# Cross-attention's 64-column products in one row per unit, contexts first in the last units

## The chip, the cores and the metric

The kernel runs on one core of a Trainium2 chip. The core has TensorE (PE: matmuls, and beside them a loader of weights), VectorE (DVE), ScalarE (ACT), GpSimd (POOL) and SyncE (SP), which issues most DMAs. They run at the same time and wait for each other by semaphores; each takes its instructions in the order in which they are queued. The metric is the device time of one execution in microseconds, the median of several runs.

## The reference, cut to what matters

A pre-norm decoder layer on x of 16 sequences of 64 tokens and 256 columns, with three parts, each added to x:

```python
x = x + self_attention(layernorm(x), ...)           # 16 heads of 128, weights as codes times scales
x = x + cross_attention(layernorm(x), ctx_512, ...)  # latent attention, below
x = x + moe(layernorm(x), ...)                       # 16 experts, 4 per token, and a shared one
```

The cross-attention, per head h of 16 (K = 128, latent query 192 wide, context 64 wide, R = 64):

```python
q_hk  = (hidden_q @ Wq.T).reshape(B, S, H, K)
q_big = rope(einsum('bshk,hkq->bshq', q_hk, w_kc_q))       # 192 wide
kv_r  = rope(kv_c)
q_r   = einsum('bshq,hqr->bhsr', q_big, W_qr)
k_r   = einsum('bld,hdr->bhlr', kv_r, W_kr)
attn  = softmax(einsum('bhsr,bhlr->bhsl', q_r, k_r))
ctx_c = einsum('bhsl,bld->bhsd', attn, kv_r)
ctx   = einsum('bhsd,hkd->bhsk', ctx_c, w_kc_kv)
return ctx.transpose(0, 2, 1, 3).reshape(B, S, H * K) @ Wo.T
```

The expert layer takes a softmax over 16 logits, picks two of four groups of experts and then four experts per token, and adds their weighted outputs and a shared expert's.

## The kernel before

**Tiling.** The 1024 tokens are eight tiles x[0] to x[7] of 128 tokens; half 0 is the first four, half 1 the rest. After a layer norm, `layernorm_t` (L159) leaves a half's rows transposed, two 128-row chunks of 512 tokens, each split in a high and a low part for float precision; a product over such parts is three matmuls (`three`, L107). PSUM has four buffers "mm", two "at" and two "av", each one bank.

**Cross-attention.** Heads go in four quads, and a quad for one half of the tokens is a unit; there are eight, in the list `units` (L1134). `quad_steps` (L403) multiplies a quad's weights together ahead of time (matmuls L431, L453, L470); for quads 2 and 3 that happens inside the units' loop, as the generator `prep`. A unit is then:

- `rotated_queries` (L975), a generator in three steps t=0, 1, 2. Each step makes two products of six matmuls of 128 columns into an mm buffer (helper line L104, called "w_q work" here, 12 matmuls a step), four multiplications by the rope table on DVE (L993, the "factors", rt), which empty the buffers, and a subtraction and an addition on POOL (L999), which make two tiles of rotated rows, `roped`.
- `pair_queries` (L1005): the queries of four heads from all six roped tiles, on 64 columns of the array per product (L1014; 24 matmuls in the trace), into two mm buffers, copied to `q_r` by ACT (L1025).
- `pair_scores` (L1029), twice, two heads each: 16 matmuls of 64 columns (L1037) into an at buffer, then `softmax` (L320): maximum, difference, (ACT) exponential, sum, reciprocal on DVE, and the final multiplication on POOL (L334), or on DVE for the last unit.
- `transposed` (L339), twice: four PE transposes (L343) and two ACT copies.
- `pair_context` (L1046), twice: 16 matmuls of 64 columns (L1050) into an av buffer, split in parts c_t by ACT (L112) and DVE (L113).
- `cross_project` (L1064): four products of six matmuls (L104, w_o), one mm buffer each, added to x by DVE (L1075).

**Staging.** The loop over n (L1138) is a software pipeline: iteration n does the rotation of unit n, the queries and scores of unit n−1, and the transposes, contexts and projection of unit n−2. Half 0 of x is complete after n=6; a third layer norm and the routing follow there: `choose(0)` (L760) is two short groups of matmuls and a long row of small DVE operations, and `send` (L846) scatters rows by POOL's DMAs. After n=9 the same is done for half 1, with the shared expert's products (`shared_up`, L909, and others) as PE's filler; then come the routed experts, whose first input rows need these sends.

**Order.** No order is written out by hand. A planner with a model of durations takes the instructions as the program issues them, earlier ones first where several are ready, and so fixes each engine's queue. `tc.issue_after(ins)` (in `after`, L95) makes instructions of the block stand behind `ins` in the queue of ins's engine, without a wait. `behind` (L249) makes a true wait on semaphores.

Of the kernel before, what the change touches and what calls it, by code (L numbers as in the profile page):

```python
# [30 lines left out]
ALU = mybir.AluOpType  # L31
# [40 lines left out]
def decoder_layer(ctx: ExitStack, tc: tile.TileContext, a: dict, out: bass.AP):  # L72
    nc = tc.nc
# [11 lines left out]
    def mm_tile(rows=128, cols=512):  # L85
        return ps_mm.tile([128, 512], F32, tag="mm", name="mm")[:rows, :cols]
# [15 lines left out]
    def matmuls(ps, pairs):  # L102
        for n, (l, r) in enumerate(pairs):
            m = nc.tensor.matmul(ps, lhsT=l, rhs=r, start=(n == 0), stop=(n == len(pairs) - 1))  # L104
        return m.ins
# [43 lines left out]
    n_pt, pn_turned = [0], []  # L149
# [99 lines left out]
    def behind(read, writes):  # L249
        for w in writes:  # L250
            tc.add_manual_dep(
                read,
                w.name,
                mybir.DependencyInfo(mybir.DependencyClass.Sync, mybir.DependencyReason.DATA),
                reason="it reads rows of each",
            )
# [58 lines left out]
    with ExitStack() as attn:  # L315
# [4 lines left out]
        def softmax(sc, scale, eng=None):  # L320

            shape = [128, 8, S]
            m = small.tile([128, 8], F32, tag="sm_m", name="sm_m")
            nc.vector.tensor_reduce(m, sc, AX.X, ALU.max)  # L324
            p = soft.tile(shape, F32, tag="p", name="p")
            nc.vector.tensor_tensor(p, sc, m.unsqueeze(2).broadcast_to(shape), ALU.subtract)  # L326
            exps.append(nc.scalar.activation(p, p, AF.Exp, scale=scale).ins)  # L327
            s = small.tile([128, 8], F32, tag="sm_s", name="sm_s")
            nc.vector.tensor_reduce(s, p, AX.X, ALU.add)  # L329
            nc.vector.reciprocal(s, s)  # L330
            pn = soft.tile(shape, F32, tag="pn", name="pn")
            softened.append(
                (eng or nc.vector)
                .tensor_tensor(pn, p, s.unsqueeze(2).broadcast_to(shape), ALU.mult)  # L334
                .ins
            )
            return pn
# [153 lines left out]
        with tc.tile_pool(name="sw", bufs=2, side="right") as sw, tc.tile_pool(name="sa", bufs=2, side="right") as sa:  # L491
# [143 lines left out]
            for h in range(NH + 3):  # L635
# [9 lines left out]
                last = []  # L645
# [86 lines left out]
        def token_rows(half):  # L732
            return [rows[half][k // 2][:, k % 2, :D] for k in range(4)]
# [234 lines left out]
        with (  # L968
# [3 lines left out]
            def rope_table(t, k):  # L972
                return rope_q[:, t, k : k + 1, :].broadcast_to([128, 8, S])

            def rotated_queries(w_q, half, roped):  # L975
                for t in range(3):
                    m = []
                    for ab in range(2):
                        ps = mm_tile()
                        cols = slice(t * 128, (t + 1) * 128)  # L980
                        pairs = []
                        for c in range(2):
                            pairs += three(
                                [w[:, c, ab, cols] for w in w_q],
                                [p[:, c, :] for p in xn_t[half]],
                            )
                        matmuls(ps, pairs)
                        ps3 = ps.rearrange("p (b s) -> p b s", s=S)
                        for k in range(2):
                            mt = xa.tile(  # L990
                                [128, 8, S], F32, tag=f"rt{ab}{k}", name=f"rt{ab}{k}"
                            )
                            nc.vector.tensor_tensor(mt, ps3, rope_table(t, 2 * ab + k), ALU.mult)  # L993
                            m.append(mt)
                    for ab, (one, two, op) in enumerate(
                        ((m[0], m[3], ALU.subtract), (m[2], m[1], ALU.add))
                    ):
                        r = xa.tile([128, 512], F32, tag=f"roped{t}{ab}", name=f"roped{t}{ab}", bufs=1)
                        nc.gpsimd.tensor_tensor(  # L999
                            r.rearrange("p (b s) -> p b s", s=S), one, two, op  # L1000
                        )
                        roped.append(r)
                    yield

            def pair_queries(w_s, roped):  # L1005
                ps = [mm_tile() for _ in range(2)]
                left = [4 if h in (1, 2) else 2 for h in range(4)]
                first = [True] * 4
                for t in range(3):
                    for ab in range(2):  # L1010
                        for blk in range(2):
                            h = BLOCK_HEADS[t][blk]
                            left[h] -= 1
                            nc.tensor.matmul(  # L1014
                                ps[h // 2][(h % 2) * 64 : (h % 2) * 64 + 64],
                                lhsT=w_s[:, t, blk, ab, :],
                                rhs=roped[2 * t + ab],
                                start=first[h],
                                stop=left[h] == 0,
                            )  # L1020
                            first[h] = False
                q_rs = []
                for pr in range(2):
                    q_r = xa.tile([128, 512], F32, tag="q_r", name="q_r", bufs=2)
                    nc.scalar.copy(q_r, ps[pr])  # L1025
                    q_rs.append(q_r)
                return q_rs

            def pair_scores(q_r, half, eng):  # L1029

                sc = at_tile([128, 8, S])
                sc4 = sc.rearrange("p (h g) s -> p h g s", h=2)
                for g in range(2):
                    for pp in range(2):
                        for par in range(2):
                            b = 4 * g + 2 * par + pp
                            nc.tensor.matmul(  # L1037
                                sc4[par * 64 : par * 64 + 64, :, 2 * g + pp, :],
                                lhsT=q_r[:, b * S : (b + 1) * S],
                                rhs=kv_bd[:, half * 8 + b],  # L1040
                                start=True,
                                stop=True,
                            )
                return softmax(sc, 1.0, eng)

            def pair_context(pt, half):  # L1046
                av = av_tile()
                for k in range(4):
                    for hp in range(2):
                        nc.tensor.matmul(  # L1050
                            av[hp * 64 : hp * 64 + 64, k * 128 : (k + 1) * 128],
                            lhsT=kv[:, half * 4 + k, :],
                            rhs=pt[:, 4 * hp + k].rearrange("p a q -> p (a q)"),
                            start=True,
                            stop=True,
                        )
                c_t = [
                    xa.tile([128, 512], F32R, tag=f"c_t{n}", name=f"c_t{n}", bufs=4)
                    for n in range(2)
                ]  # L1060
                parts_of(av, c_t[0], c_t[1])
                return c_t

            def cross_project(w_o, c_ts, half, last):  # L1064
                for k in range(4):
# [69 lines left out]
            late = {1: quad_steps(2, weights, xb), 3: quad_steps(3, weights, xw)}  # L1135
            prep = iter(())
            roped, pns = {}, {}
            for n in range(len(units) + 2):  # L1138
                here = range(len(units))
                if n in late:  # L1140
# [2 lines left out]
                roped[n] = []  # L1143
                qd, half = units[min(n, len(units) - 1)]
                rotate = iter(rotated_queries(weights[qd][0], half, roped[n]) if n in here else ())
                pts_n = [transposed(pn) for pn in pns.pop(n - 2, ())]
                if n - 1 in here:
                    q_rs = pair_queries(weights[units[n - 1][0]][1], roped.pop(n - 1))
                c_ts = [pair_context(pt, units[n - 2][1]) for pt in pts_n]
                next(rotate, None)  # L1150
                if n - 1 in here:

                    eng = nc.gpsimd if n < len(units) else nc.vector
                    pns[n - 1] = [pair_scores(q_rs[0], units[n - 1][1], eng)]
                if n in late:
                    next(prep)
                next(rotate, None)
                if n == 0:
                    with tc.issue_after(highs[-1]), tc.issue_after(lows[-1]):
                        xn_t += layernorm_t(2, (1,))  # L1160
                if n - 1 in here:
                    pns[n - 1].append(pair_scores(q_rs[1], units[n - 1][1], eng))
                if n in late:
                    next(prep)
                if n - 2 in here:
# [24 lines left out]
                    )  # L1190
                if n == 6:
                    rows[0] = [raw_tile(tag, [128, 2, ROW]) for tag in ("wq", "wkq")]
                    normed[0] = layernorm_t(3, (0,), token_rows(0))[0]
                if n == 7:
                    choose(0)
                    send(0, (0, 1))
# [333 lines left out]
```

## Time and profile before

| | |
|---|---|
| median of 3 runs | 562.55 us (560.79 to 564.96) |
| the profiled execution, its own time | 559.35 us |
| its span | 557.5 us |
| PE, weight loader | 526.9 us (95%), 440.0 us (79%) |
| DVE, ACT, POOL | 398.9 us (72%), 276.9 us (50%), 230.3 us (41%) |
| mean granted PE clock | 0.984 |
| cross-attention, by the first and last of its matmuls | 204.4 to 409.2 us |

A span is counted from the first instruction of the trace to the last, and times in the text are from its start. Busy time of PE is that of matmuls in flight, which overlap: a matmul of 512 columns is recorded with about 0.40 us, while the next starts 0.23 us after it. So what tells a lost moment on PE is the distance between starts. "Issue" is a wait that the profile has no releaser for. In rows, "128\*64" is the part of the array that a matmul uses, rows by columns.

### The profile page before, as it was taken

What the parts mean: (1) busy time and instruction counts of PE and PEld (TensorE: products, weight loads), DVE (VectorE), ACT (ScalarE), POOL (GpSimd) and SP (SyncE); (2) the same over time, 40 slices, a digit from 0 to 9 for tenths busy, and PEclk for the clock granted to TensorE, in tenths of its full rate; (3) what the DMA queues carried; (4) which work ended last, traced back from release to release, by engine and by line L of the source; (5) the groups of instructions that cost most, each with busy time, mean ns of one, the idle gap of its engine ahead of it and who ended that gap; (6) DMA issues with size and microseconds to landing.
All of it is one profiled execution on the core that took longest, in us unless ns stands there. A gap on an engine that the chain in (4) does not pass through costs nothing.

```text
span 557.5 us, 10620 instructions
## 1 busy us (share of the span) xinstructions
PE 526.9 (95%) x4013; PEld 440.0 (79%) x4013; DVE 398.9 (72%) x879; ACT 276.9 (50%) x524; POOL 230.3 (41%) x213
## 2 busy tenths in 40 slices
PE   7999999999999989999999999999999789999961
PEld 6898898998999965756778577685788679999951
DVE  5464574664746888846768496889778679999776
ACT  4677557576574511321332323143535468776551
POOL 4360510210101015516344443642545737888862
PEclk9999999999999999999999999999999989999995
DMA  8453431923201889280020000010512677676375
GB/s 255 152 178 108 126 104 54 235 86 115 77 1 37 263 240 288 80 243 13 1 68 6 8 1 1 0 31 1 166 67 83 208 252 252 233 251 227 136 258 176
DMA packets 44262, 70.83 MB, mean 127 GB/s; under 512 B 11824, under 2 KB 25232, under 8 KB 44208
## 3 DMA queue, kind: packets, MB, share of 16 engines
q1 hardware_dynamic: 39376, 58.71, 34.8%
q0 software_dynamic: 3696, 10.36, 4.8%
q10 hardware_dynamic: 1136, 1.05, 0.6%
q8 instruction: 33, 0.54, 0.4%
q14 instruction: 21, 0.17, 0.1%
HBM read 48.61 MB, written 21.86 MB: 126 GB/s over the span
## 4 chain that ended last, share of the span: by engine, by line
PE 77%; DVE 9%; POOL 4%; issue 3%; DMA 3%; ACT 3%; SPq 0%; DVEq 0%; POOLq 0%; ACTq 0%
PE mm L104 45%; PE mm L1014 7%; PE av L592 5%; PE av L104 3%; PE at L573 3%; PE at L343 3%; PE at L1037 2%; POOL xd L851 2%; PE av L1050 2%; PE mm L431 2%; PE mm L453 1%; ACT w L278 1%; DMA got<-yd 1%; DVE x L1343 1%; PE at L1274 1%
## 5 line engine op out<-in xcount | busy, mean ns | idle before, releaser
L999 POOL TENSOR_TENSOR roped<-rt,rt 128x512 f32<-128x512 f32 x48 | 62.6, 1325 | 83.0 <-DVE rt L993 80.1
L993 DVE TENSOR_TENSOR rt<-mm,rope_q 128x512 f32<-128x512 f32 x96 | 61.4, 685 | 24.1 <-PE mm L104 23.6
L104 PE MATMUL mm<-xn,w_q 128*128 128x512 f32 x288 | 73.9, 403 | 0.5 <-ACT xn L222 0.5
L104 PEld LDWEIGHTS mm<-xn,w_q 128*128 128x128 f32 x288 | 52.2, 188 | 14.0 <-issue 1.8
L104 PE MATMUL mm<-xs,w 128*128 128x384 f32 x270 | 54.2, 348 | 5.0 <-ACT xs L112 2.7
L1313 POOL DMA_INDIRECT yd<-y,to x45 | 47.8, 1062 | 20.8 <-ACT y L1308 8.3
L104 PEld LDWEIGHTS mm<-xs,w 128*128 128x128 f32 x270 | 47.0, 193 | 7.2 <-ACT xs L112 3.7
L324 DVE TENSOR_REDUCE sm_m<-at 128x8 f32<-128x512 f32 x32 | 21.8, 680 | 43.1 <-PE at L573 42.2
L1014 PE MATMUL mm<-roped,w_s 128*64 128x512 f32 x192 | 46.4, 602 | 0.7 <-POOL roped L999 0.7
L514 POOL TENSOR_TENSOR wv<-code,scale 128x512 fp32r<-128x512 f32 x7 | 10.3, 1471 | 88.4 <-DMA code<-in_codes 45.2
L327 ACT ACTIVATE p<-p 128x512 f32<-128x512 f32 x32 | 20.4, 636 | 38.6 <-DVE p L326 38.6
L329 DVE TENSOR_REDUCE sm_s<-p 128x8 f32<-128x512 f32 x32 | 21.9, 683 | 21.1 <-ACT p L327 21.1
L104 PE MATMUL mm<-wv,xn 128*128 128x256 f32 x256 | 36.2, 289 | 0.0
L104 PE MATMUL av<-w,hp 128*128 128x256 f32 x225 | 35.1, 289 | 0.4 <-ACT y L1308 0.3
L104 PE MATMUL mm<-xn,wk 128*128 128x512 f32 x128 | 34.3, 399 | 0.0
L351 ACT COPY pt<-at 64x512 f32<-64x512 f32 x32 | 18.5, 579 | 30.8 <-PE at L343 30.7
L104 PE MATMUL mm<-xn,wq 128*128 128x512 f32 x128 | 33.2, 398 | 0.2
L104 PEld LDWEIGHTS mm<-wv,xn 128*128 128x128 f32 x256 | 32.5, 189 | 0.7
L104 PE MATMUL mm<-wo,o 128*128 128x256 f32 x256 | 33.0, 285 | 0.0
L601 ACT ACTIVATE o<-av,bqkv 128x512 fp32r<-128x512 f32 x32 | 21.3, 688 | 23.0 <-PE mm L104 19.0
L1014 PEld LDWEIGHTS mm<-roped,w_s 128*64 128x64 f32 x192 | 13.9, 136 | 22.9 <-issue 20.5
L104 PEld LDWEIGHTS mm<-wo,o 128*128 128x128 f32 x256 | 31.4, 191 | 0.7 <-issue 0.4
(216 smaller groups left out, 1169.1 us busy)
## 6 DMA issues: line engine op xcount, KB each, us to landing
w<-in_W SPq DMA_DIRECT2D x15, 640.0 KB, 4.3
code<-in_codes SPq DMA_DIRECT2D x32, 256.0 KB, 4.5
scale<-in_scales SPq DMA_DIRECT2D x32, 256.0 KB, 4.8
xr<-xd SPq DMA_DIRECT2D x15, 408.0 KB, 4.8
xd<-zeros SPq DMA_DIRECT2D x8, 720.0 KB, 7.1
yd<-zeros SPq DMA_DIRECT2D x8, 512.0 KB, 6.8
got<-yd SPq DMA_DIRECT2D x16, 256.0 KB, 3.8
wq<-in_Wq SPq DMA_DIRECT2D x4, 512.0 KB, 4.6
```

The source lines that it names most:

```text
L104: m = nc.tensor.matmul(ps, lhsT=l, rhs=r, start=(n == 0), stop=(n == len(pairs) - 1))
L324: nc.vector.tensor_reduce(m, sc, AX.X, ALU.max)
L327: exps.append(nc.scalar.activation(p, p, AF.Exp, scale=scale).ins)
L329: nc.vector.tensor_reduce(s, p, AX.X, ALU.add)
L343: last = nc.tensor.transpose(ps[:, 2 * n : 2 * n + 2, :].rearrange("p a q -> p (a q)"), pn[:, 2 * n : 2 * n + 2, :].rearrange("p a k -> p ...
L351: nc.scalar.copy(pt[:S, :, 0, :], ps[:S])
L592: nc.tensor.matmul(av[:, k * 128 : (k + 1) * 128], lhsT=v[:, i, k0 : k0 + HD], rhs=pt[:, i].rearrange("p a q -> p (a q)"), start=True, sto ...
L601: nc.scalar.activation(o[0][:, cols], av, AF.Identity, bias=bias)
L993: nc.vector.tensor_tensor(mt, ps3, rope_table(t, 2 * ab + k), ALU.mult)
L999: nc.gpsimd.tensor_tensor(r.rearrange("p (b s) -> p b s", s=S), one, two, op)
L1014: nc.tensor.matmul(ps[h // 2][(h % 2) * 64 : (h % 2) * 64 + 64], lhsT=w_s[:, t, blk, ab, :], rhs=roped[2 * t + ab], start=first[h], stop=l ...
L1313: sent = nc.gpsimd.indirect_dma_start(out=yd[: (E - 1) * SLOTS + min(TOPK, E - 1 - e) * NT], out_offset=bass.IndirectOffsetOnAxis(ap=to[:, ...
```

## The change

In each iteration the order of PE's work is now bound:

1. The transposes of unit n−2 stand behind the last projection product of the iteration before (for n < 8).
2. t=0 of unit n's rotation comes first; the queries of unit n−1 stand behind its last matmul and (n > 2) behind the transposes. The first query product also waits, truly, for the last DVE factor of unit n−1 (`roped_done`; not in n=8).
3. The contexts of unit n−2, both, stand behind the queries; both scores behind the contexts; preparation and t=1 behind the scores. Before, the scores of the two pairs had t=1 between them, and the planner was free.
4. For n = 7 and above contexts come ahead of the queries. The layer norm of half 0 for the experts moves from the end of n=6 to n=7, behind these contexts.

```diff
@@ rotated_queries @@
-                        matmuls(ps, pairs)
+                        asked = matmuls(ps, pairs)
...
-                            nc.vector.tensor_tensor(mt, ps3, rope_table(t, 2 * ab + k), ALU.mult)
+                            factors = nc.vector.tensor_tensor(
+                                mt, ps3, rope_table(t, 2 * ab + k), ALU.mult
+                            )
...
-                    yield
+                    roped_last[0] = factors.ins
+                    yield asked
@@ pair_queries @@
+                behind(products[0], roped_done)
...
-                return q_rs
+                return q_rs, products[-1]
@@ the loop over n @@
-                pts_n = [transposed(pn) for pn in pns.pop(n - 2, ())]
+                with after(*([projected] if n < len(units) and projected else [])):
+                    pts_n = [transposed(pn) for pn in pns.pop(n - 2, ())]
+                roped_done = list(roped_last)
+                order = [m for m in [next(rotate, None)] if m]
+                c_ts = []
+
+                def contexts(order):
+                    for pt in pts_n:
+                        with after(*order):
+                            c_t, product = pair_context(pt, units[n - 2][1])
+                        order = [product]
+                        c_ts.append(c_t)
+                    return order
+
+                if n >= 7:
+                    order = contexts(order)
+                if n == 7:
+                    with after(*order):
+                        normed[0] = layernorm_t(3, (0,), token_rows(0))[0]
                 if n - 1 in here:
-                    q_rs = pair_queries(weights[units[n - 1][0]][1], roped.pop(n - 1))
-                c_ts = [pair_context(pt, units[n - 2][1]) for pt in pts_n]
-                next(rotate, None)
-                if n - 1 in here:
-                    eng = nc.gpsimd if n < len(units) else nc.vector
-                    pns[n - 1] = [pair_scores(q_rs[0], units[n - 1][1], eng)]
-                if n in late:
-                    next(prep)
-                next(rotate, None)
+                    with after(*order, *([pn_turned[0]] if n > 2 else [])):
+                        q_rs, product = pair_queries(
+                            weights[units[n - 1][0]][1],
+                            roped.pop(n - 1),
+                            roped_done if n < len(units) else [],
+                        )
+                    order = [product]
+                if n < 7:
+                    order = contexts(order)
                 if n == 0:
                     with tc.issue_after(highs[-1]), tc.issue_after(lows[-1]):
                         xn_t += layernorm_t(2, (1,))
                 if n - 1 in here:
-                    pns[n - 1].append(pair_scores(q_rs[1], units[n - 1][1], eng))
+                    eng = nc.gpsimd if n < len(units) else nc.vector
+                    pns[n - 1] = []
+                    for q_r in q_rs:
+                        with after(*order):
+                            pn, product = pair_scores(q_r, units[n - 1][1], eng)
+                        order = [product]
+                        pns[n - 1].append(pn)
+                if n in late:
+                    with after(*order):
+                        next(prep)
+                with after(*order):
+                    next(rotate, None)
...
                 if n == 6:
                     rows[0] = [raw_tile(tag, [128, 2, ROW]) for tag in ("wq", "wkq")]
-                    normed[0] = layernorm_t(3, (0,), token_rows(0))[0]
```

More of the change, by code (lines that the diff above doesn't have):

```diff
@@ L1002, in rotated_queries, with pair_queries @@
                         roped.append(r)
-                    yield
-            def pair_queries(w_s, roped):
-                ps = [mm_tile() for _ in range(2)]
+                    roped_last[0] = factors.ins
+                    yield asked
+            def pair_queries(w_s, roped, roped_done):
+                ps, products = [mm_tile() for _ in range(2)], []
                 left = [4 if h in (1, 2) else 2 for h in range(4)]
@@ L1013, in pair_queries @@
                             left[h] -= 1
[L1014 to L1019, printed above, removed]
+                            products.append(
+                                nc.tensor.matmul(
+                                    ps[h // 2][(h % 2) * 64 : (h % 2) * 64 + 64],
+                                    lhsT=w_s[:, t, blk, ab, :],
+                                    rhs=roped[2 * t + ab],
+                                    start=first[h],
+                                    stop=left[h] == 0,
+                                ).ins
                             )
                             first[h] = False
+                behind(products[0], roped_done)
                 q_rs = []
@@ L1036, in pair_scores @@
                             b = 4 * g + 2 * par + pp
-                            nc.tensor.matmul(
+                            last = nc.tensor.matmul(
                                 sc4[par * 64 : par * 64 + 64, :, 2 * g + pp, :],
@@ L1043, in pair_scores @@
                             )
-                return softmax(sc, 1.0, eng)
+                return softmax(sc, 1.0, eng), last.ins
             def pair_context(pt, half):
@@ L1049, in pair_context @@
                     for hp in range(2):
-                        nc.tensor.matmul(
+                        last = nc.tensor.matmul(
                             av[hp * 64 : hp * 64 + 64, k * 128 : (k + 1) * 128],
@@ L1061, in pair_context @@
                 parts_of(av, c_t[0], c_t[1])
-                return c_t
+                return c_t, last.ins
             def cross_project(w_o, c_ts, half, last):
@@ L1137, in decoder_layer @@
             roped, pns = {}, {}
+            roped_last, projected = [None], None
             for n in range(len(units) + 2):
```

## The prediction

> **What bounds the kernel now.** I read the page first (a matmul in flight for 95% of the span, 77% of the ending chain on PE), then cut the cross-attention stage into stretches of about one unit each: length, each engine's busy time, granted clock, DMA share, GB/s.
>
> ```profile
> core 0: us, PE busy (x) PEld busy (x) DVE busy (x) ACT busy (x) POOL busy (x), PEclk, DMA share, GB/s
> ...
> 309.00:332.00 23.00, 23.00 (x160) 15.52 (x158) 14.69 (x28) 7.19 (x13) 8.94 (x8) 1.00 0.02 5
> 332.00:354.00 22.00, 22.00 (x158) 15.46 (x159) 16.84 (x31) 7.13 (x12) 11.01 (x8) 1.00 0.00 1
> 354.00:379.00 25.00, 25.00 (x187) 18.64 (x184) 19.44 (x52) 10.27 (x18) 11.56 (x10) 1.00 0.06 18
> 379.00:410.00 31.00, 29.77 (x225) 21.49 (x224) 26.64 (x91) 13.19 (x22) 11.32 (x10) 1.00 0.26 87
> ```
>
> See: up to 379 us PE never rests, at full clock, beside DVE at 64 to 78%. A busy PE isn't a PE at its peak, so I then looked at single starts, in the timeline of matmuls and, separately, of weight loads, where a 64-column product stands between 128-column ones:
>
> ```profile
> 345.79 1.10 PE L104 MATMUL mm<-xn,w_q 128*128 128x512 f32 x4
> 346.82 1.09 PE L1037 MATMUL at<-kv_bd,q_r 128*64 128x128 f32 x16
> 347.84 0.73 PE L104 MATMUL mm<-w_o,c_t 128*128 128x256 f32 x4
> ```
> ```profile
> 346.82 0.85 PEld L1037 LDWEIGHTS at<-kv_bd,q_r 128*64 128x64 f32 x16 [0.37 <-issue]
> 347.84 0.65 PEld L104 LDWEIGHTS mm<-w_o,c_t 128*128 128x128 f32 x5 [0.17 <-issue]
> ```
>
> See: the loader stops for 0.37 us before the 64-column group and 0.17 us after it, waiting for nothing the trace names. Those holes are what the change is about. From 379 on it is a chain of latencies; in the chain of waits:
>
> ```profile
> 382.74 1.17 DVE limit L787
> ...
> 387.71 0.61 DVE p L326
> 388.32 0.02 issue
> 388.34 0.64 ACT p L327
> ...
> 394.81 1.09 PE av L1050 x16
> 395.91 2.99 PE mm L104 x12
> ```
>
> See: DVE alternates the last softmax with the routing (choose), and PE fills with the shared expert.
>
> **The price of one switch.** Four w_q matmuls take 1.10 us, the last 0.40: three starts in 0.70, 0.233 each. The fourth starts at 346.49, the scores at 346.82: 0.33, so entering costs 0.10. Eight pairs of score products take 1.09, the last 0.28: 0.81 for seven steps, where inside a row a step is 0.109: 0.05 more, all in the first step. Last pair 347.63 to w_o at 347.84: 0.20 instead of 0.11, leaving costs 0.09. The first w_o step is 0.22 instead of 0.12: 0.10. Round trip 0.34 us (0.29 when it leaves to transposes, whose first step is 0.17 for 0.11). Two rules bear on this. The Trainium skill ("TensorE: Matmul & The Clock Gate", section "Step-by-step: what each phase is for") says PE pulls weight loads ahead of matmuls in flight; were that whole, a switch would be free and the change worth nothing. "TensorEngine Tiling (Array Packing)", section "Key Properties", says a change of tiling mode drains TensorE; draining exposes 0.40 − 0.233 = 0.165 per switch, 0.33 both ways. The row decides for the second.
>
> **How many go.** Stretches of 64 columns or fewer in the matmul timeline: 5, 4, 4, 4, 3, 3, 4 in the iterations n=1 to 7 (27 by 379 us) and 6 from there to 404. After: one each for n=1 to 6, one or two for n=7 (the layer norm's transposes can come between), and about three for the quad preparations (L453, L470), whose place isn't bound: 10. At the end, context+queries+scores of n=8 in one or two, the last two contexts one each: 4. So 17 go before 379 us, at 0.32 (between 0.29 and 0.34) 5.4 us; two later, 0.6 us.
>
> **What it adds: waits.** (a) The first query product waits for DVE's last factor of that unit. Queued behind it on PE: contexts, scores, t=1, projection; behind those ACT's q_r copies and DVE's softmax. In before the last factor ended 1.3 to 2.3 us after its unit's last w_q matmul (e.g. 333.26 for 331.94, 356.02 for 353.76; unit 0 4.0). In front of the queries now stands t=0 of the next unit: 12 × 0.233 and a switch, 3.0 us. So 0 for units 1 to 6; for unit 0 about 1 us, which equals the two waits for POOL there now (0.2 and 0.5 us idle, 1.0 with their delayed starts). Cover gone, it costs each unit what DVE is late beyond 3.0. (b) POOL's last rows: two operations after the factor, 2.5 us, ended 3.4 to 5.1 us after the last w_q matmul; the products that need them come at 3.0 + 8 pairs × 0.43 = 6.5. Hidden. (c) Scores behind contexts: 1.75 us of contexts cover the q_r copy (0.59); in n=7 and 8, where contexts go first, the first q_r is complete eight products early and the second copy hides behind the first scores (1.0 us). The 0.6 us wait at 383.68 goes. (d) Transposes ahead of the queries need both pn: softmax is four DVE steps (2.2 us), 0.63 on ACT, 1.04 on POOL, some 5 to 7 us, against 9 us of PE work (t=1, projection, t=2): hidden. In n=7 and 8 contexts follow their transposes by two ACT copies (1.2 us): t=0 covers it in n=7; in n=8 between 0 and 1.2, I take 0.4.
>
> (e) What I price worst: scores now come together instead of 3 us of t=1 apart. DVE then owes at once two c_t parts (0.69), two maxima and two differences (0.68 each), 4.1 us, while PE goes on to t=1 and the projection's four tiles, six allocations on four PSUM buffers. From the end of scores, T: differences done T+1.8, factors of t=1 T+3.1, a sum and reciprocal, second factors T+5.3; PE wants those buffers back at T+4.5 and T+5.25, and t=2 wants the first x addition (T+6.0, or T+6.6 behind a sum) at T+6.0. So 0 to 0.6 us per unit if DVE's order is kind, 1 to 1.5 if both sums come first. The skill's Tiling page, section "PSUM Bottleneck", warns of just this, that tiling speeds TensorE and not the emptying of PSUM; by the rule DVE would set the pace in every unit and the gain be gone; but the stretches show DVE at 64 to 78%, so it catches up. I take 0.2 for six units, 1.2 us.
>
> (f) The layer norm of half 0 moves from the end of n=6 into n=7. Its instructions are the same: eight transposes, eight DVE statistics, one POOL power (1.0 us), ACT and DVE scalings. No DMA moves; what is behind it on POOL (rows, softmax products) is shifted by that 1.0 us at most, under t=0. SP's queue isn't passed; POOL's sends still follow choose. Between −0.5 and +0.5; zero.
>
> **Sum.** To the end of the last unit's w_q work: −5.4 + 1.2 = −4.2. From there two paths matter. PE's own work: −0.6 switches, −0.6 at q_r, +0.4: −0.8 more. The chain queries, scores, softmax, context, layer norm, choose, sends: its second scores end at 389.2 in before; now 379.35 + 1.85 (contexts ahead) + 5.65 (queries) + 2.05 (scores) = 388.9, less the gain so far. After that the softmax took 8.7 us (to 397.94) for about 5.5 of work, since it was interleaved with choose; now choose, begun as early, is mostly behind: 1 to 3 us less. So the chain gains about 6, PE 5.0. Expert 0's rows arrive (idle 0.55 on PE at 436.6) just as PE ends its filler, so the smaller counts: −5.0. The profiled execution took 559.35 (span 557.5 + 1.85): 554.35. It lay 3.2 under the median of the runs, so 562.55 − 5.0 = **557.5**.
>
> **Rivals.** *DVE holds PSUM* (slower, 0.2): place, the projection and t=2 after each double score; price, 1.4 us in units 1 to 6, 8.5 in all, against 6 won: +2.5, 565. It decides from 0.9 to 1 us per unit. For it: the 4.1 us burst, and 1.97 us for a 128x704 subtraction at 333.98, beside POOL's rows, where its twin took 0.88. Against: no wait over 0.14 us on PE from 230 to 379 us now. *The end profits more* (0.25): with contexts first the last chain loses 3 to 5 us and PE's filler moves into the holes between 436 and 455 us (some 5 us): −8, 554.5. For it: the interleaving above; against: PE is full from 409 to 430 us. *It doesn't stay in a row* (0.12): the ordering only binds named products; transposes, preparation, layer norm and gating may be placed between by the planner. Half the switches remain: −2, 560.5.
>
> **How the numbers follow.** Likeliest 0.43: 557.5, by itself 556 to 559.5 (0.29 or 0.34 per trip, waits 0 to 2.5 us). Leaving out the outer part of each rival: 553.8 to 565. One per cent is 5.6 us, about what a measurement can tell from no change: faster by more has most of the second rival and a third of the likeliest, 0.37; slower by more needs 1.9 us lost in every unit: 0.09; else 0.54.
>
> **What would show it.** One 64-column stretch per unit from n=2, about 14 in all; t=0 directly before the queries; no PE wait on L993 in units 1 to 6; units some 0.7 us shorter; PE not waiting on L1075 or L993 in the projection; the last x addition 5 to 7 us earlier than 409.99. It is wrong if the queries wait for DVE, if PE waits for PSUM after the scores, or if the sends start no earlier.

## The result and the profile after

The changed kernel took 572.48 us (median of four runs, 570.78 to 574.62), the kernel before 563.75 us in the same comparison; the ratio on record is 1.0134, 95% interval 1.0087 to 1.0182 (the two medians alone give 1.0155, inside it). It is slower by 1.3%. Some executions of a kernel, whatever the kernel, take over 1.5% longer than its fastest; all ratios here compare the others alone. Forecast was 557.5 us, at most 565. The profiled execution took 570.78 us, its span 569.0 us: 11.5 us more than the span before. The profiled execution before took 559.35 us, less than each of the four that 563.75 is the median of, so the two profiles lie further apart than the medians.

The stretches of the cross-attention stage after the change (length, busy time per engine, granted clock, DMA share, GB/s):

```profile
core 0: us, PE busy (x) PEld busy (x) DVE busy (x) ACT busy (x) POOL busy (x), PEclk, DMA share, GB/s
309.00:332.00 23.00, 22.09 (x161) 16.61 (x160) 14.75 (x28) 7.55 (x14) 9.13 (x8) 1.00 0.02 5
332.00:354.00 22.00, 21.09 (x157) 15.51 (x156) 18.16 (x36) 6.38 (x11) 10.25 (x8) 1.00 0.00 1
354.00:379.00 25.00, 24.47 (x182) 17.82 (x180) 18.38 (x51) 7.74 (x14) 10.55 (x9) 1.00 0.06 17
379.00:420.40 41.40, 32.72 (x223) 23.90 (x224) 26.20 (x83) 14.32 (x25) 11.23 (x10) 0.88 0.18 66
```

PE now rests 0.9 us in each of the first two stretches and 0.5 in the third; the last has 8.7 us of rest and a clock of 0.88. Who PE waited for, longest in total first (us, times, longest):

```profile
PE av L806 <- DVE sel L749: 5.6, 1, 5.6
PE mm L104 <- DVE rt L993: 3.8, 5, 0.9
PE at L343 <- DVE r_s L890: 1.8, 1, 1.8
PE at L343 <- DVE r_p L891: 0.7, 1, 0.7
PE av L1057 <- DVE over L834: 0.5, 1, 0.5
PE av L1057 <- ACT pt L352: 0.5, 1, 0.5
```

All are new; the two large ones are what follows is about. Neither is the wait that the change names: no line has the first query product waiting for the last factor.

To see where the time went, the span is cut at four events of the traces: the first w_q matmul, the last one, the end of the last addition to half 1 of x, and the first send of half 1's rows.

| kernel | first to last w_q start | to the last addition to x | to the first send of half 1 | to the end of the span |
|---|---|---|---|---|
| before | 174.6 | 31.0 | 16.0 | 131.5 |
| after | 173.1 | 42.7 | 17.5 | 131.1 |

So the units up to the last w_q matmul won 1.5 us, not 4.2, and the end lost 11.7 instead of winning 0.8. The 1.5 us in the third column are a DVE pause of 1.69 us in the second choose, whose cause the trace doesn't name; the run without the true wait (below), whose work there is the same, has 16.0, so I don't put it to the change.

The matmul timeline at the end shows the loss itself (start, length, count, idle time before it and who ended it):

```profile
377.96 1.04 PE L343 MATMUL at<-ident,pn 128*128 128x128 f32 x8
384.62 0.69 PE L806 MATMUL av<-sel,upto 128*128 128x64 f32 x2 [5.62 <-DVE sel L749]
385.24 1.98 PE L1057 MATMUL av<-pt,kv 128*64 128x128 f32 x16
387.14 0.69 PE L807 MATMUL av<-before,ones 128*128 128x64 f32 x2
388.37 1.97 PE L1057 MATMUL av<-pt,kv 128*64 128x128 f32 x16 [0.54 <-DVE over L834]
390.11 6.91 PE L1019 MATMUL mm<-roped,w_s 128*64 128x512 f32 x24
```

L806 and L807 are the placing matmuls of choose(0) (tokens counted per expert). The planner queued L806 directly behind the transposes and ahead of the contexts; it needs `sel`, the result of a long row of DVE operations. Contexts, and behind them the last queries, stood 5.6 us in a queue for work that they don't need. In the kernel before, L806 came behind the last queries, when `sel` was ready (at 385.7 us), and waited for nothing:

```profile
384.60 1.89 PE L1014 MATMUL mm<-roped,w_s 128*64 128x512 f32 x8
386.42 0.44 PE L806 MATMUL av<-sel,upto 128*128 128x64 f32 x2
386.78 1.09 PE L1050 MATMUL av<-pt,kv 128*64 128x128 f32 x16
```

After the wait PE also ran slowly: sixteen context matmuls in 1.98 us, 1.09 before; the queries in 6.91 us, about 5.4 in every other unit. The clock of these moments:

```profile
378.00:384.50 6.50, 0.99 (x9) 0.75 (x7) 6.29 (x29) 2.97 (x5) 3.29 (x2) 0.89 0.00 0
384.50:394.00 9.50, 8.84 (x48) 5.71 (x50) 4.97 (x26) 1.17 (x2) 3.00 (x3) 0.54 0.08 31
394.00:397.00 3.00, 3.00 (x16) 0.82 (x11) 0.00 (x0) 0.58 (x1) 2.08 (x4) 1.00 0.25 93
384.70:393.20 8.50, 7.96 (x44) 5.31 (x46) 4.80 (x25) 1.17 (x2) 2.20 (x3) 0.50 0.05 18
```

The last row, inside the second, shows a low clock of one half; so the first two rows hold 1.4 and 8.7 us of it. Cost, estimated from the lengths above: 2 × 0.9 + 1.5, some 3.3 us.

In the units the other wait recurs at the projection's last tile. The projection of n=2 in the kernel before ran without a pause:

```profile
253.78 3.14 PE L104 MATMUL mm<-w_o,c_t 128*128 128x256 f32 x24
```

In the changed kernel, matmuls, then DVE, of n=2:

```profile
248.31 3.06 PE L104 MATMUL mm<-xn,w_q 128*128 128x512 f32 x12
251.21 2.31 PE L104 MATMUL mm<-w_o,c_t 128*128 128x256 f32 x18
254.43 0.95 PE L104 MATMUL mm<-w_o,c_t 128*128 128x256 f32 x6 [0.91 <-DVE rt L993]
```
```profile
249.95 0.69 DVE L326 TENSOR_TENSOR p<-at,sm_m 128x512 f32<-128x512 f32 x1
250.56 0.68 DVE L329 TENSOR_REDUCE sm_s<-p 128x8 f32<-128x512 f32 x1
251.15 1.28 DVE L993 TENSOR_TENSOR rt<-mm,rope_q 128x512 f32<-128x512 f32 x2
252.34 0.19 DVE L330 RECIPROCAL sm_s<-sm_s 128x8 f32<-128x8 f32 x1
252.45 0.64 DVE L329 TENSOR_REDUCE sm_s<-p 128x8 f32<-128x512 f32 x1
253.00 1.28 DVE L993 TENSOR_TENSOR rt<-mm,rope_q 128x512 f32<-128x512 f32 x2
```

The fourth tile needs the PSUM buffer that the second pair of t=1 factors empties, and these stand behind the sums of both softmaxes, one ahead of each pair of factors. A step of w_o is 0.12 us; here it is 1.19.

### The profile page after: what moved, and what is told of

It reads as the page before. It is cut to its first block, busy times and chain, and to the rows that moved or that the text cites. A ratio compares the mean times of both kernels' runs of the same rounds, so it can differ in the third digit from the quotient of the medians.

```text
span 569.0 us, 10615 instructions
## 1 busy us (share of the span) xinstructions
PE 526.1 (92%) x4013; PEld 444.2 (78%) x4013; DVE 402.3 (71%) x879; ACT 276.3 (49%) x524; POOL 228.1 (40%) x213
## 4 chain that ended last, share of the span: by engine, by line
## 5 line engine op out<-in xcount | busy, mean ns | idle before, releaser
L1019 PE MATMUL mm<-roped,w_s 128*64 128x512 f32 x192 | 44.6, 614 | 0.0
L514 POOL TENSOR_TENSOR wv<-code,scale 128x512 fp32r<-128x512 f32 x7 | 9.0, 1292 | 86.4 <-DMA code<-in_codes 43.6
L334 POOL TENSOR_TENSOR pn<-p,sm_s 128x512 f32<-128x512 f32 x14 | 14.6, 1046 | 47.2 <-DVE sm_s L330 47.2
L104 PEld LDWEIGHTS av<-w,hp 128*128 128x128 f32 x225 | 31.0, 193 | 1.7 <-ACT y L1347 1.2
```

The costliest lines, as they stand in the source:

```text
L514: mults[n] = eng.tensor_tensor(w, *loaded[gr].pop(n), ALU.mult).ins
L1019: nc.tensor.matmul(ps[h // 2][(h % 2) * 64 : (h % 2) * 64 + 64], lhsT=w_s[:, t, blk, ab, :], rhs=roped[2 * t + ab], start=first[h], stop=l ...
```

## The experiments

Three theories. **1**: the placing matmul, queued ahead of the contexts, and the low clock after it, are the loss. **2**: DVE's softmax sums hold PSUM in the projection and take back what the switches give. **3** (rival): the order itself costs, by the true wait or by contexts being first. In each edit `...` marks lines left out.

**Placing matmuls behind the last queries.** `choose` is cut before its placing matmuls; these, all of `choose` that follows them, and the sends are issued in n=8 after `pair_queries`:

```diff
                 if n == 7:
-                    choose(0)
-                    send(0, (0, 1))
+                    placing = choose_steps(0, [])
+                    next(placing)
...
+                if n == 8:
+                    with after(*order):
+                        for _ in placing:
+                            pass
+                    send(0, (0, 1))
```

> The changed kernel with the second part of choose(0), from its placing matmuls on, issued in n=8 behind the last unit's queries on PE (sends after it). Theory 1 (the placing matmul stands ahead of the contexts in PE's queue and holds contexts and queries of the last units for 5.6 us, and PE then runs at half clock): no wait over 1 us on PE between 376 and 392 us, clock 1.0 there, 8 to 11 us less than the changed kernel, 562 to 565. Theory 2 alone (PSUM held by DVE's sums in the projection): at most 1 us less, 571.5. Theory 3 (contexts first and the wait for the last factor are themselves the loss): unchanged, 572.

Measured: 1.0021 of the kernel before (1.0005 to 1.0038), 561.29 against 559.87 us. PE there:

```profile
380.80 1.03 PE L343 MATMUL at<-ident,pn 128*128 128x128 f32 x8
382.74 2.30 PE L1064 MATMUL av<-pt,kv 128*64 128x128 f32 x32 [0.91 <-ACT pt L352]
384.87 3.60 PE L1026 MATMUL mm<-roped,w_s 128*64 128x512 f32 x16
```

The wait of 5.6 us is gone, the queries run at their usual pace, and x is complete 35.0 us after the last w_q start instead of 42.7. By the ratios that is 1.1% or 6.4 us, less than the 8 to 11 expected; against the run without the true wait (below), which was measured beside this one and has the same two large waits as the changed kernel, it is 8.2 us. Two waits for ACT's copies of pt are left in the end (0.9 and 1.7 us). The clock is 1.00 from 376 to 392 us, as expected, but behind the second of these waits, from 402.5 us, it is one half for 3.4 us. Theory 1 carries most of the loss.

**The wait filled.** 52 idle transposes (of the identity, into a buffer that nobody reads) stand behind the transposes of pn and ahead of the placing matmuls, and contexts behind both of these:

```diff
+                if n == 8:
+                    busy = av_tile()
+                    with after(pn_turned[0]):
+                        for k in range(52):
+                            turn = nc.tensor.transpose(
+                                busy[:, k % 4 * 128 : k % 4 * 128 + 128], ident, ident
+                            )
+                    with after(turn.ins):
+                        for _ in placing:
+                            pass
+                    send(0, (0, 1))
+                    order = [of_choice[0][1]]
...
```

> The changed kernel with 52 idle transposes on PE (5.7 us) between the last but one unit's transposes and the placing matmul, which stay ahead of the contexts; they fill the wait of 5.6 us and end no later than it. If the idle stretch is what lowers the clock: granted clock 1.0 from 384 to 394 us, contexts 1.0 instead of 2.0 us each, queries 5.3 instead of 6.9, 3 to 3.5 us less, 569. If the low clock has another cause: contexts and queries as long as before, 572 or more.

Measured: 1.0089 (1.0063 to 1.0115), 565.0 us. Its timeline and its clock:

```profile
378.89 5.84 PE L1182 MATMUL av<-ident 128*128 128x128 f32 x52
384.81 0.41 PE L813 MATMUL av<-sel,upto 128*128 128x64 f32 x2
385.61 0.43 PE L814 MATMUL av<-before,ones 128*128 128x64 f32 x2 [0.40 <-DVE before L808]
385.98 1.97 PE L1064 MATMUL av<-pt,kv 128*64 128x128 f32 x32
387.77 5.32 PE L1026 MATMUL mm<-roped,w_s 128*64 128x512 f32 x24
```
```profile
384.50:394.00 9.50, 9.03 (x71) 4.96 (x69) 5.03 (x26) 2.34 (x4) 4.08 (x4) 1.00 0.12 45
```

The contexts start no earlier than in the changed kernel, both take 1.97 us together instead of 1.98 each, and the queries 5.32. The queries end 3.9 us sooner and x is complete 4.9 us sooner, of 7.7 with the placing matmuls behind. In the time this is 0.45% by the ratios to the kernel before (2.5 us), with intervals that overlap; against the run without the true wait, measured beside it, it is 4.5 us (1.0089 against 1.0182), clear of the noise. So useless work in the gap makes the kernel faster: the idle stretch brings the low clock. A little of the gain, up to 0.5 us, is another matter: L807 no longer stands between the contexts, and the wait for `over` behind it is gone.

**Sums behind the factors.** The softmax's second part (sum, reciprocal, last multiplication) is issued after t=1:

```diff
-                return softmax(sc, 1.0, eng), last.ins
+                return softmax_begun(sc, 1.0), last.ins
...
+                if n - 1 in here:
+                    with after(*(roped_last if n in here else ())):
+                        pns[n - 1] = [softmax_rest(p, eng) for p in begun_sm]
```

> The changed kernel with sum, reciprocal and last multiplication of both softmaxes issued behind the factors of t=1 on DVE. Theory 2: the waits of the projection's last tile (five, 0.9 us idle each, 1.07 over the usual step) go, 4 to 5 us less by the last unit's rotation; in the time 567.5 to 568.5 if the end is shifted with it. Theory 1: the wait of 5.6 us at the placing matmul stays, and may take part of this back (then 569 to 572). Theory 3: 572.

Measured: 1.0116 (1.0083 to 1.0149), 565.72 us: no clear difference from the changed kernel's ratio. A miss in size. The waits for the factors went, but others took their place:

```profile
PE av L812 <- DVE sel L755: 5.6, 1, 5.6
PE mm L104 <- DVE x L1088: 1.7, 4, 0.5
```

The first w_q matmuls of t=2 now wait 0.4 to 0.5 us for the additions to x, which stand behind the sums. From first to last w_q it is 171.6 us, 1.5 less than in the changed kernel and not 4 to 5. Theory 2 has the right place, but the sums, moved back, made the additions late instead.

**Without the true wait.**

```diff
-                behind(products[0], roped_done)
```

> The changed kernel without the true wait of the first query product for VectorE's last factor (the products still wait for their own rows). Theories 1 and 2: no change, 572 plus or minus 1, since the profile shows no PE wait there. Theory 3 (the wait is what costs): 3 us or more less, 569 or below.

Measured: 1.0182 (1.0131 to 1.0234), no better than the change itself; first to last w_q 173.3 us. The true wait costs nothing that can be seen, as forecast. That half of theory 3 falls.

The next four were measured beside each other where the kernel before took from 566.82 to 576.30 us, so that their intervals are wide. **The changed kernel again**, without an edit:

> The changed kernel itself once more, beside the others on the same chip: 1.013 times the kernel before, wait of 5.6 us at the placing matmul.

Measured: 1.0115 (1.0018 to 1.0212). **Queries first in the last units too**, with choose untouched:

```diff
-                if n >= 7:
-                    order = contexts(order)
...
-                if n < 7:
-                    order = contexts(order)
+                order = contexts(order)
```

> The changed kernel with contexts behind the queries in the last units too, choose untouched. Theory 1: the planner now puts the placing matmul behind the last queries, which take 5.3 us, about as long as choose needs; no wait over 1 us there, clock 1.0, 5 to 8 us less than the changed kernel. Theory 3 (it is the ordering in a row, not the placing matmul's place): at most 1 us less.

Measured: 1.0051 (0.9966 to 1.0137). The placing matmul came behind the queries and no longer waits, as theory 1 has it; x is complete 36.7 us after the last w_q start (44.4 in the changed kernel of this group). The interval leaves the size open. In the trace the gain, 7.7 us, is the same as with the placing matmuls moved. **Both edits**, placing and sums:

> Placing matmuls behind the last queries and sums behind the factors of t=1 together. If the two causes add: the first alone gave some 7.5 us and the second some 3.5 us, 11 in all, which is the whole loss and a little more: 0.995 to 1.000 of the kernel before. If they hide each other: no better than the first alone, 1.002.

Measured: 1.0062 (0.9933 to 1.0191): undecided. **Scores first**, that is sums behind the factors, and in n=8 queries, scores, contexts (the call stands after the scores and binds nothing; the planner put some of the contexts between the two scores, the rest behind):

```diff
-                if n >= 7:
+                if n in (7, 9):
                     order = contexts(order)
...
+                if n == 8:
+                    contexts([])
```

> Sums behind factors, and in n=8 queries, then scores, then contexts, with choose untouched. The planner has the placing matmul behind the first scores. The last chain starts its softmax earliest of all: scores end 2 us sooner than with contexts ahead, nothing waits over 1 us: 0.988 to 0.996 of the kernel before. If choose on DVE is what the softmax waits for, no better than 1.000.

Measured: 0.9955 (0.9854 to 1.0055): undecided. These last two once more, where the kernel before was steadier:

> Placing matmuls behind the last queries and sums behind the factors, taken again for the same reason. If the causes add: 0.995 to 1.000; if they hide each other: 1.002, as the first alone.

Measured: 1.0007 (0.9988 to 1.0026), 560.28 us: a draw, and the interval holds both expectations, 1.000 and 1.002. In the trace the two gains stand side by side: 171.6 us as with the sums alone, 35.0 as with the placing matmuls alone.

> The same edit as the earlier run with scores ahead of contexts in n=8 and sums behind the factors, taken again because that chip was disturbed. If both losses are gone and the switches' 5 us stay won: 0.988 to 0.997 of the kernel before. If contexts' and scores' order at the end gives nothing: 1.000.

Measured: 0.996 (0.9946 to 0.9973), 557.6 us. From the run with the sums behind (1.0116) this one differs in a single thing, the place of n=8's contexts in the program, behind the last scores; choose is untouched. With it the planner put the placing matmul behind the first scores, without a wait, and x is complete 31.8 us after the last w_q start instead of 40.6, near the 31.0 of before. So it is the contexts' place that let the placing matmul in.

From the run with both edits, where x is complete 35.0 us after the last w_q start, it differs in the end alone: in the place of these contexts, and in that the rest of choose isn't moved. PE, with scores first:

```profile
377.38 1.04 PE L349 MATMUL at<-ident,pn 128*128 128x128 f32 x8
378.34 3.65 PE L1025 MATMUL mm<-roped,w_s 128*64 128x512 f32 x16
```

The queries start 1.0 us after the transposes, against 4.1 with contexts ahead (380.80 to 384.87 in the rows of the first experiment; the same in the run with both edits). So contexts first cost about 3 us beside what the placing matmul did: their own length and a wait of 0.9 us for pt. The other half of theory 3 stands, as a third cause. How it divides is open: with queries alone ahead of the contexts, as above, x was complete no sooner than with the placing matmuls moved, but that run has other waits in its end.

**Additions first.** With scores first, the sums of n=2 to 7 are issued behind the projection's last addition:

```diff
...
+                if n in range(2, 8):
+                    with after(added[0]):
+                        pns[n - 1] = [softmax_rest(p, eng) for p in begun_sm]
```

> As with scores first, and the sums of n=2 to 7 issued only behind the projection's additions to x on DVE. If the rest of the waits in the projection (0.5 us idle, four times, for the additions) comes from sums ahead of them, these go and the last rotation ends 2 us sooner: 2 us under the run with scores first. If the later sums then hold up the transposes, which stand ahead of the queries, a wait for them appears and nothing is won.

Measured: 0.9923 (0.9902 to 0.9943), 556.27 us: the 2 us that were expected, but by luck, from two terms that were not. First to last w_q fell to 168.1 us, 3.5 less and not 2: from the first w_q matmul of one unit to that of the next, units 2 to 6 became 0.7, 1.0, 0.3, 0.7 and 0.7 us shorter, which is more than the idle time of the waits that went (0.3 to 0.5 us each); the rest isn't traced. And the last but one unit's transposes now waited for pn, 2.1 us of x's completion. Hence **additions first in n=2 to 6 only** (`range(2, 7)`):

> As with the additions first, but only in n=2 to 6; in n=7 the sums stay behind the factors, so that the last but one unit's transposes don't come late to the end. In the run with n=2 to 7 two PE waits for pn (0.8 and 1.1 us over the usual step) stood behind the last rotation, and x was complete 34.0 us after it, against 31.8 without. If these were the price: 32 us again, 1 to 2 us less, 0.989 to 0.991. If the wait of the projection at n=7 comes back for it: 0.992 as before.

Measured: 0.9879 (0.9852 to 0.9907), 552.96 against 559.86 us: faster than both kernels, by a little more than expected. Its DVE in n=2, to be laid beside the rows of the changed kernel above:

```profile
251.25 0.69 DVE L328 TENSOR_TENSOR p<-at,sm_m 128x512 f32<-128x512 f32 x1
251.85 2.47 DVE L999 TENSOR_TENSOR rt<-mm,rope_q 128x512 f32<-128x512 f32 x4
254.25 1.07 DVE L1088 TENSOR_TENSOR x<-mm,x 128x256 f32<-128x256 f32 x3
255.59 0.42 DVE L1088 TENSOR_TENSOR x<-mm,x 128x256 f32<-128x256 f32 x1 [0.27 <-PE mm L104]
255.93 1.27 DVE L335 TENSOR_REDUCE sm_s<-p 128x8 f32<-128x512 f32 x2
```

Here the four factors come in a row, where the changed kernel had a sum ahead of each pair, and both sums behind the additions: what PE waits for comes before what only the next unit needs. In n=7, where nothing binds the sums in this run, DVE had them between the two pairs of factors, and PE did not wait for it there.

| kernel | first to last w_q start | to the last addition to x | ratio |
|---|---|---|---|
| before | 174.6 | 31.0 | 1 |
| after | 173.1 | 42.7 | 1.0134 |
| placing behind | 173.1 | 35.0 | 1.0021 |
| wait filled | 173.1 | 37.8 | 1.0089 |
| sums behind | 171.6 | 40.6 | 1.0116 |
| both | 171.6 | 35.0 | 1.0007 |
| scores first | 171.6 | 31.8 | 0.996 |
| additions first, n=2 to 7 | 168.1 | 34.0 | 0.9923 |
| additions first, n=2 to 6 | 168.0 | 31.8 | 0.9879 |

## Why the prediction was wrong

**The price of a switch and their number: right, nearly.** Twelve stretches of 64 columns or fewer are left before the last w_q matmul, where 10 were forecast; 15 of 27 went, at 0.32 to 0.34 us 4.8 to 5.1 us. The best run is a check on it: 6.6 us less from first to last w_q than before, of which 0.9 are eight transposes that now come after the last w_q work. PE's waits in between are about the same in both (0.7 and 0.6 us), so about 5.6 are left, a little more than the count gives; the rest isn't traced.

**(a) and (b), waits for factors and rows: right.** No query product in units 1 to 6 waits, and the run without the true wait is no faster.

**(e), double scores and PSUM: right place, wrong size.** I took 0.2 us per unit and had both ends in hand, 0.6 for a kind order of DVE and 1 to 1.5 for both sums first. What came is priced like the second: one sum ahead of each pair of factors, so both ahead of the second pair, 1.07 us over the usual step four times and 0.75 in n=3, 5.0 us in place of 1.2. That alone is about what the switches won. (d) added 0.7: in n=7 the contexts did wait for pt, which t=0 was to cover. What is left of the gain comes from the two waits that vanished at unit 0 (1.0 with their delayed starts) and the transposes that moved (0.9): 5.1 + 1.0 + 0.9 − 5.0 − 0.7 = 1.3 us, where 1.5 was measured. The doubt should have gone the other way, since nothing in the change makes the planner put factors ahead of sums that come earlier in the program.

**The chain at the end: wrong, and the larger loss, 11.7 us where 0.8 were to be won.** The step that failed is "now choose, begun as early, is mostly behind: 1 to 3 us less". It counted choose as work on DVE only. Choose also has two matmuls on PE, and while contexts stood behind nothing in n=8 (their `order` is empty, since there is no rotation), the planner was free to put L806 ahead of them. I named such an intrusion, in the rival that the row doesn't stay whole, and priced it at switches of 0.3 us; its price was the wait of whatever the intruder waits for, 5.6 us, and some 3.3 us of low clock after it, a term that the sum didn't have. The order in n=8 failed too: contexts ahead of the last queries were to cost 1.85 us, to be paid back later, with 0.4 for pt; pt took 0.9, and even without the placing matmul the end is about 3 us longer than with scores ahead.

**The rivals.** The slower one had a true mechanism, PSUM held by DVE, and too high a price, 8.5 us where 5.0 came; it did not make the kernel slower alone, since first to last w_q is still 1.5 us shorter than before. The mechanism that decided, the wait of a matmul queued ahead and the clock behind it, was in no rival.

## What to carry to other kernels

When an order binds some instructions of a queue, ask what the unbound ones do: each that the planner may put ahead can cost not only its own length but its wait, and a matmul that depends on a long row of small operations belongs behind everything that doesn't. Packing products that share a mode is worth what single starts say, but it bunches their consumers; on the consuming engine, put what frees the producer's buffers first and what only a later unit needs last. After a stall of PE, price the slow stretch that follows it as well.

## What the hardware showed that was not expected

In an idle stretch of 5.6 us PE's clock fell to one half, and it stayed there for about 10 us, the first 1.4 of them still idle; full speed came back only in the middle of the queries: 3.3 us on top of the wait. The run with idle transposes in the gap has 1.00 from 378 to 397 us. The trace of the kernel before has no low clock in the cross-attention stage. The Trainium skill warns of it ("TensorE: Matmul & The Clock Gate", section "HAM oscillation — how this bites in real kernels": no PE-idle gaps over about 3.4 us); the stretch of 5.6 us agrees with that. Shorter waits did not always spare the clock, though, and here the measurement decides: waits of up to 0.9 us in the units left it at 1.00, but with the placing matmuls behind, a wait of 1.7 us was followed by 3.4 us at one half, while one of 1.8 us in the changed kernel, at 407 us, was not. The clock behind the wait of 1.7 us:

```profile
402.60:405.90 3.30, 3.30 (x14) 2.58 (x11) 1.58 (x4) 2.40 (x4) 2.34 (x3) 0.50 0.71 212
```

So no length of wait that is safe can be read from these runs.
